# Two GNN layers on one core: h1's two right-hand products as one joint two-level product, W1 from DRAM, x1 added by the DMA

## The chip, the core and the metric

The kernel runs on one core of a Trainium2 chip. A core has TensorE (PE, matrix products into PSUM), VectorE (DVE), ScalarE (ACT), GpSimd (POOL) and SyncE (SP, which here issues most DMAs); they run their own instruction streams in program order and wait for one another by semaphores. The metric is the time of one execution in microseconds on the device (us). The kernel before was run three times: median 2367.68, from 2367.29 to 2368.17.

## The reference

Everything is fp32. There are 32 batches of 512 nodes with 512 features, an adjacency `adj` (512x512 per batch) and a node mask.

```python
h = relu(layernorm(x))                       # over the features
deg = adj.sum(-1)
agg = adj @ h / max(deg, 1e-6)
x1 = x + relu(concat(h, agg) @ W.T)          # W: 512 x 1024
h1 = relu(layernorm(x1))
q, k = split(h1 @ Wqk)
v = h1 @ Wv
w = mask * sum(q * (adj @ (k * mask)), -1) / sqrt(512)
out = x1 + softmax(w, over the nodes) * v
```

## The kernel before, in words

**Algebra.** W is split in W1 (for h) and W2 (for agg). With A = adj/deg the kernel computes y = h·W2 and out = h·W1 + A·y. In the second layer the weights of q and k are joined before the loop, M = Wq·Wkᵀ, so that the score of a node is the dot product of a row of t = h1·M with the same row of u = A·(mask·h1), times the degree. So a batch has six 512x512x512 terms: y, h·W1, A·y, u, t and v = h1·Wv.

**Products.** Each term is a Strassen-Winograd product over 2x2 blocks of 256: seven block products, each of four matmuls of 128x128 weights with 256 moving columns (28 matmuls instead of 32). The weights come from a transposed left operand (hT, aT, h1T, sums of blocks included: seven slots), the moving columns from a right operand with seven slots. `product` (L114) is a generator that yields after each step of four matmuls per term; the matmul is L124. Its banks are pp, pr and pq. Their order: block product 1 into pp, copied by ScalarE (L91) as c11; 2 into pr, added by VectorE (L85); 6 is accumulated onto pp, hence waits for the copy of pp; then 5 into pq (copied as m5), 7 onto pp, 3 onto pq, 4 onto pp. Sums of blocks for a left or a right operand are four VectorE operations of 128x512 each (L85 add, L88 subtract). Where a result becomes the right operand of another product (y), `end` in `layer0_y` makes its sums on VectorE.

**Transposes.** A normalised row block goes to a DRAM scratch tensor, is read back so that 32-blocks lie where they are wanted, and is transposed by VectorE in 32x32 blocks (L199). This is done for h, A and h1 (classes `FrontH` L263, `FrontA` L283, `FrontH1` L310).

**Stages.** The order of the work is written out by hand: for each stage a plan lists what else is issued after which step (`at(step, f)`), and `run` (L158) takes a step of the products, then what the plan has there. A batch i has three stages: SINGLE, out(i), 14 steps; PAIR, t(i-1) and v(i-1) with steps interleaved; PAIR, y(i+1) and u(i) interleaved. The chain from out to h1 (statistics L221 and L222, variance L226, power -0.5 on POOL L227, shift L231, normalisation with ReLU on ScalarE L235, mask L331) is issued in the t/v stage. Softmax (L404 and following) with its two reductions over partitions on POOL comes in the y/u stage; there VectorE adds sm·v to x1 in the x tile (L437), and SP stores it (L444). W1, W2, M and Wv stay in SBUF as `w1R`, `w2R`, `mR`, `vR` for the whole kernel. DMAs are issued by SP, in order.

**Head and tail.** Before the loop the weights are turned, M is multiplied (`pm`), and out(0) runs; between them TensorE transposes the mask (L622). After the loop the last softmax, its additions and stores follow the last product of v.

## Time and profile before

| | |
|---|---|
| median of three runs | 2367.68 us |
| profiled execution, its own time | 2370.62 us |
| its span (first to last instruction) | 2368.8 us |
| granted TensorE clock, mean | 0.998 |
| TensorE busy | 2343.9 us |
| VectorE busy | 1491.9 us |
| ScalarE busy | 861.2 us |
| POOL busy | 91.9 us |
| moved by the SP queue | 335.74 MB, 56.2% of 16 DMA engines |
| one batch in mid-run (1072 to 1146 us and 1000 to 1072) | 72 to 74 us |
| end of the last matmul to the end of the span | about 6.9 us |

The profile is of one execution, a little apart from the median. An instruction group's row gives line, engine, operation, tile written and tiles read, shape, count, then busy time and mean ns of one, then the idle time of the engine ahead of the group and what ended it. A matmul instruction leaves two records, so that "x8" is four matmuls; their lengths overlap, and the distance of the starts is the pitch. The timeline's rows are start, length, instruction, with the idle time before it and its releaser in brackets. Of a wait for several things the row names the last.

### The profile page before, as it was taken

The page shows a single profiled execution, that of the slowest core. Times are in us where ns is not written, and L with a number is a line of the kernel's source. Part 1 is how long each engine was busy: PE and PEld are TensorE (multiplying, and loading weights), DVE is VectorE, ACT ScalarE, POOL GpSimd, SP SyncE. Part 2 cuts the span into 40 slices and gives each one's busy share as a digit, 9 for nine tenths or more (in the row PEclk, how much of TensorE's full clock was granted, in tenths as well). Part 3 has the DMA queues.
Part 4 walks back from the last instruction along what each step waited for, and adds up shares of the span by engine and source line. Part 5 has one row for each costly group of instructions (what it writes and reads, how often), then busy time and mean ns, then how long its engine had stood idle before and what let it go on. Part 6 is the DMA issues. An engine that isn't in the chain of part 4 may idle for free.

```text
span 2368.8 us, 31069 instructions
## 1 busy us (share of the span) xinstructions
PE 2343.9 (99%) x10916; PEld 2063.5 (87%) x10916; DVE 1491.9 (63%) x3132; ACT 861.2 (36%) x1555; POOL 91.9 (4%) x134
## 2 busy tenths in 40 slices
PE   6999999999999999999999999999999999999998
PEld 5988888888888888888888888888888888888887
DVE  5676665666666666666666666666666666666544
ACT  4443333343333433333433334333344333343322
POOL 0000000000000000000000000000000000000000
PEclk9999999999999999999999999999999999999999
DMA  8864656645655546556456564465564665645412
GB/s 158 217 187 122 155 152 144 158 128 131 175 146 143 139 128 161 147 141 160 128 138 171 147 145 137 124 166 143 142 159 122 147 166 146 149 133 128 116 38 69
DMA packets 363596, 337.72 MB, mean 143 GB/s; under 512 B 32656, under 2 KB 266128, under 8 KB 363440
## 3 DMA queue, kind: packets, MB, share of 16 engines
q1 hardware_dynamic: 363440, 335.74, 56.2%
q8 instruction: 86, 1.41, 0.3%
q14 instruction: 70, 0.57, 0.1%
HBM read 203.49 MB, written 132.12 MB: 142 GB/s over the span
## 4 chain that ended last, share of the span: by engine, by line
PE 97%; DMA 1%; DVE 0%; ACT 0%; SPq 0%; POOL 0%; issue 0%; DVEq 0%; ACTq 0%
PE pp_o L124 19%; PE pp_v L124 9%; PE pp_t L124 9%; PE pq_o L124 9%; PE pp_u L124 9%; PE pp_y L124 9%; PE pq_v L124 5%; PE pq_t L124 5%; PE pq_y L124 5%; PE pq_u L124 5%; PE pr_o L124 5%; PE pr_v L124 2%; PE pr_t L124 2%; PE pr_u L124 2%; PE pr_y L124 2%; DMA n<-in_x_dram 0%
## 5 line engine op out<-in xcount | busy, mean ns | idle before, releaser
L124 PE MATMUL pp_o<-w1R,hT 128*128 128x256 f32 x1024 | 243.4, 381 | 0.0
L124 PE MATMUL pp_y<-w2R,hT 128*128 128x256 f32 x1024 | 242.5, 380 | 0.0
L124 PE MATMUL pp_t<-mR,h1T 128*128 128x256 f32 x1024 | 241.9, 379 | 0.0
L124 PE MATMUL pp_o<-y,aT 128*128 128x256 f32 x1024 | 241.9, 379 | 0.0
L124 PE MATMUL pp_v<-vR,h1T 128*128 128x256 f32 x1024 | 241.9, 379 | 0.0
L124 PE MATMUL pp_u<-h1m,aT 128*128 128x256 f32 x1024 | 241.9, 379 | 0.0
L124 PEld LDWEIGHTS pp_o<-w1R,hT 128*128 128x128 f32 x1024 | 195.4, 191 | 26.8
L124 PEld LDWEIGHTS pp_y<-w2R,hT 128*128 128x128 f32 x1024 | 194.9, 191 | 26.4
L124 PEld LDWEIGHTS pp_u<-h1m,aT 128*128 128x128 f32 x1024 | 194.6, 190 | 26.5
L124 PEld LDWEIGHTS pp_t<-mR,h1T 128*128 128x128 f32 x1024 | 194.6, 190 | 26.5
L124 PEld LDWEIGHTS pp_v<-vR,h1T 128*128 128x128 f32 x1024 | 194.6, 190 | 26.5
L124 PEld LDWEIGHTS pp_o<-y,aT 128*128 128x128 f32 x1024 | 194.5, 190 | 26.4
L91 ACT ACTIVATE o<-pp_o 128x512 f32<-128x512 f32 x96 | 57.3, 597 | 371.8 <-PE pp_o L124 371.8
L235 ACT ACTIVATE h1m<-x,nmr,rstd 128x512 f32<-128x512 f32 x128 | 99.9, 806 | 171.9 <-DVE nmr L231 171.9
L91 ACT ACTIVATE v<-pp_v 128x512 f32<-128x512 f32 x128 | 75.5, 590 | 223.5 <-PE pp_v L124 223.5
L91 ACT ACTIVATE y<-pp_y 128x512 f32<-128x512 f32 x128 | 76.4, 597 | 205.6 <-PE pp_y L124 205.6
L199 DVE STREAM_TRANSPOSE aT<-saT 128x1024 f32<-128x1024 f32 x62 | 77.2, 1245 | 114.3 <-DMA saT<-daT 92.6
L91 ACT ACTIVATE u<-pp_u 128x512 f32<-128x512 f32 x128 | 76.2, 595 | 141.2 <-PE pp_u L124 141.2
L227 POOL TENSOR_TENSOR rstd<-rstd,mhalf 128x4 f32<-128x4 f32 x64 | 66.6, 1040 | 1553.2 <-ACT m_o L91 913.5
L124 PE MATMUL pq_y<-w2R,hT 128*128 128x256 f32 x512 | 121.1, 379 | 0.1
L124 PE MATMUL pq_t<-mR,h1T 128*128 128x256 f32 x512 | 121.0, 379 | 0.0
L124 PE MATMUL pq_o<-y,aT 128*128 128x256 f32 x512 | 121.0, 379 | 0.0
(115 smaller groups left out, 3753.0 us busy)
## 6 DMA issues: line engine op xcount, KB each, us to landing
x<-in_x_dram SPq DMA_DIRECT2D x128, 256.0 KB, 5.6
a<-in_adj_dram SPq DMA_DIRECT2D x256, 128.0 KB, 3.1
dh1T<-h1m SPq DMA_DIRECT2D x128, 256.0 KB, 2.5
sh1T<-dh1T SPq DMA_DIRECT2D x256, 128.0 KB, 3.5
out_dram<-x SPq DMA_DIRECT2D x256, 128.0 KB, 2.3
n<-in_x_dram SPq DMA_DIRECT2D x248, 128.0 KB, 4.7
daT<-a SPq DMA_DIRECT2D x124, 256.0 KB, 2.0
dhT<-n SPq DMA_DIRECT2D x124, 256.0 KB, 2.0
```

The source lines that it names most:

```text
L91: nc.scalar.activation(o, i, AF.Copy)
L124: nc.tensor.matmul(p[:, rc, :], lt[:, LEFT[k], dk, ts(rc, P)], rt[:, RIGHT[k], dk, :], start=first and n == 0, stop=True, skip_group_check ...
L199: nc.vector.transpose(o, t.rearrange("p k (c r) -> p k c r", r=R))
L227: nc.gpsimd.tensor_tensor(rstd, rstd, mhalf, op=ALU.pow)
L235: nc.scalar.activation(o, i, AF.Relu, scale=t[1][:, c:c + 1], bias=t[2][:, c:c + 1])
```

## The change

- **Joint product.** t and v are computed by `layer1_tv`: the right operand `mvR` has M and Wv side by side, 128 columns each, in blocks of 128, and the algorithm is applied twice, 7 x 7 block products of 128. Each is one matmul of 128x128 weights with 256 columns (128 of M, 128 of Wv). An outer block product fills four PSUM banks (two inner products each, one in the last); ScalarE and VectorE gather the outer sums from the banks into a tile TV, where the seven inner products of each block are still apart. h1T gets the sums of the inner level too (`inner_sums`, VectorE).
- **Recombination.** In the next stage VectorE combines the inner products by seven adds of 128x1024 (`recombine`) and makes four dot products (`dot`) of 128x512.
- **Output.** ScalarE multiplies v by the softmax weight into a tile of the tag n (`apply`), POOL issues a DMA that adds x1 from DRAM to it (`store`, two of 512 KB per batch), and SP stores it with four DMAs each. x1 is put into DRAM by `keep` (1 MB, SP).
- **W1** is kept in DRAM and loaded per batch, seven DMAs of 256 KB, three tiles (`Stream`).
- **Buffers and engines.** hT is one constant tile; aT and x have one buffer instead of two, n two instead of three, tmp four instead of five. The left sums of A and the right sums of y are made by POOL.
- **Order.** Products run one after the other: out(i) 14 steps, y(i+1) 7 steps, u(i) 7 steps, joint product tv(i) 14 half steps. The rest of the chain to h1 (`chain`) is issued in y(i+1), four masks and the reading back included; the softmax of the batch before is issued in out(i). In the last batch there is no y, and `chain` is issued alone.
- **Head.** The mask's transposes by TensorE come in the stage in which M is multiplied, and y(1) and out(0) come with other loads beside them.

The diff, cut to its core, with the indentation reduced by four. Of the old stages, described above, only removed functions are shown.

```diff
--- before.py
+++ after.py
 ...
 def block(name):
-    return big.tile([P, 2, H], F32, tag="tmp", bufs=5, name=name)
+    return big.tile([P, 2, H], F32, tag="tmp", bufs=4, name=name)
 ...
+def add(o, a, b, on=None):
+    (on or nc.vector).tensor_tensor(o, a, b, op=ALU.add)
+def sub(o, a, b, on=None):
+    (on or nc.vector).tensor_tensor(o, a, b, op=ALU.subtract)
 ...
+def left_sums(s, on=None):
     return [
-        lambda: add(s(4), s(2), s(3)), lambda: sub(s(6), s(0), s(2)),
-        lambda: sub(s(5), s(4), s(0)), lambda: sub(s(2), s(1), s(5)),
+        lambda: add(s(4), s(2), s(3), on), lambda: sub(s(6), s(0), s(2), on),
+        lambda: sub(s(5), s(4), s(0), on), lambda: sub(s(2), s(1), s(5), on),
     ]
 ...
+def variance(t, a=0, b=C):
     mv, rstd, nmr = t
-    nc.vector.tensor_scalar(rstd, mv[:, :, 1], LN_EPS, None, op0=ALU.add)
-    nc.gpsimd.tensor_tensor(rstd, rstd, mhalf, op=ALU.pow)
-def shift(t):
+    nc.vector.tensor_scalar(rstd[:, a:b], mv[:, a:b, 1], LN_EPS, None, op0=ALU.add)
+    nc.gpsimd.tensor_tensor(rstd[:, a:b], rstd[:, a:b], mhalf[:, a:b], op=ALU.pow)
+def shift(t, a=0, b=C):
 ...
+    def keep(self):
+        nc.sync.dma_start(out=self.x1.rearrange("c p f -> p c f"), in_=X[self.b])
 ...
+    def masked_sums(self, i):
+        right_sums(of(H1M[self.b]))[i]()
+    def turn(self, h):
+        if h == 0:
+            H1T[self.b] = big.tile([P, 7, 7, P], F32, tag="h1T", bufs=1, name=f"h1T_{self.b}")
+        for a in range(2):
+            self.to.turn_slot(h, a, H1T[self.b][:, 2 * h + a, 0:4, :].rearrange("p i f -> p (i f)"))
     def sums(self, i):
-        right_sums(H1M[self.b])[i]()
+        left_sums(lambda s: H1T[self.b][:, s, 0:4, :])[i]()
+    def inner_sums(self, i, a, b):
+        swap = {0: 0, 1: 2, 2: 1, 3: 3, 4: 4, 5: 5, 6: 6}
+        left_sums(lambda s: H1T[self.b][:, a:b, swap[s], :])[i]()
 ...
+    def load(self):
+        k = ORDER[self.n % 7]
+        t = big.tile([P, 2, H], F32, tag="w1", bufs=3, name=f"w1_{self.n}")
+        nc.sync.dma_start(out=t, in_=self.d[RIGHT[k]])
+        self.tiles.append((k, t))
+        self.n += 1
 ...
-    place, finish = into(y)
-    def end(r, c, o, p, s):
-        finish(r, c, o, p, s)
-        t = right_sums(y)
-        if (r, c) == (0, 1):
-            for f in t[:3]:
-                f()
-        elif (r, c) == (1, 0):
-            t[3]()
-    return product(f"y_{b}", [(HT[b], w2R)], place, end)
-def layer0_out(b):
+    return product(f"y_{b}", [(hT, right(w2R))], *into(y))
+def layer0_out(b, w1):
     def place(r, c):
         return block(f"o_{b}_{r}{c}")
@@ -370,52 +431,103 @@
             p = o
         nc.vector.scalar_tensor_tensor(dst, p, 0.0, dst, op0=ALU.max, op1=ALU.add)
-    return product(f"o_{b}", [(HT[b], w1R), (AT[b], Y[b])], place, finish)
+    return product(f"o_{b}", [(hT, w1), (AT_[b], right(Y[b]))], place, finish)
 ...
-def layer1_t(b):
 ...
-        for rc in range(2):
-            nc.vector.scalar_tensor_tensor(
-                o[:, rc, :], p[:, rc, :], 1.0, U[b][:, 2 * r + c, rc, :],
-                op0=ALU.mult, op1=ALU.mult,
-                accum_out=acc[:, c, 2 * r + rc:2 * r + rc + 1],
-            )
-    return product(f"t_{b}", [(H1T[b], mR)], place, finish)
-def layer1_v(b):
-    v = V[b] = big.tile([P, 4, 2, H], F32, tag="v", bufs=1, name=f"v_{b}")
-    return product(f"v_{b}", [(H1T[b], vR)], *into(v))
 ...
+    return product(f"u_{b}", [(AT_[b], right(H1M[b]))], *into(u))
+def layer1_tv(b):
+    t = TV[b] = big.tile([P, 4, 2, 7, P], F32, tag="h1m", bufs=1, name=f"tv_{b}")
+    left = H1T[b]
+    def m(k, banks, first):
+        for half in ((2, 1), (3, 0)):
+            for n in half:
+                if first:
+                    banks[n] = mm_tile(f"ptv_{b}_{k}_{n}")
+                for i, p in enumerate(range(2 * n, min(2 * n + 2, 7))):
+                    j = AT[p]
+                    nc.tensor.matmul(
+                        banks[n][:, :, ts(i, P)],
+                        left[:, LEFT[k], LEFT_IN[j], :],
+                        mvR[:, RIGHT[k], RIGHT[j], :, :],
+                        start=first and i == 0,
+                        stop=True,
+                        skip_group_check=True,
+                    )
+            yield half
 ...
+    def keep(o):
+        return lambda n, p: copy(part(o, n), p)
+    def plus(o):
+        return lambda n, p: add(part(o, n), p, part(o, n))
+    pp, pr, pq, m5 = {}, {}, {}, {}
+    def keep5(n, p):
+        m5[n] = block(f"m5_tv_{b}_{n}")[:, :, 0:P * min(2, 7 - 2 * n)]
+        copy(m5[n], p)
+    yield from parts(1, pp, True, keep(0))
+    yield from parts(2, pr, True, plus(0))
+    yield from parts(6, pp, False, keep(1))
+    yield from parts(5, pq, True, keep5)
+    yield from parts(7, pp, False, keep(3))
+    for n in range(4):
+        add(part(3, n), part(3, n), m5[n])
+    yield from parts(3, pq, False, plus(1))
+    yield from parts(4, pp, False, keep(2))
 ...
+    def recombine(self, i, first=0, end=4, a=0, b=2):
+        def s(j):
+            t = TV[self.b][:, first:end, a:b, PLACE[j], :]
+            return t.rearrange("p o a f -> p (o a) f") if b - a == 2 else t[:, :, 0, :]
+        o, x1, x2 = [(2, 1, 2), (1, 1, 6), (5, 1, 5), (3, 5, 3), (6, 1, 7), (7, 5, 7), (4, 6, 4)][i]
+        add(s(o), s(x1), s(x2))
 ...
+    def dot(self, c):
+        v = self.row(c, 0)
+        u = U[self.b][:, 2 * (c // 2):2 * (c // 2) + 2, c % 2, :]
+        nc.vector.scalar_tensor_tensor(
+            v, v, 1.0, u, op0=ALU.mult, op1=ALU.mult, accum_out=self.acc[:, c:c + 1]
+        )
 ...
     def apply(self, c):
-        o = X[self.b][:, c, :].rearrange("p (a f) -> p a f", a=2)
-        nc.vector.scalar_tensor_tensor(
-            o, V[self.b][:, 2 * (c // 2):2 * (c // 2) + 2, c % 2, :], self.sm[:, c:c + 1], o,
-            op0=ALU.mult, op1=ALU.add,
+        h = c // 2
+        if c % 2 == 0:
+            self.n[h] = half_tile(f"out_{self.b}_{h}")
+        nc.scalar.activation(
+            self.n[h][:, c % 2, :].rearrange("p (a f) -> p a f", a=2), self.row(c, 1), AF.Copy,
+            scale=self.sm[:, c:c + 1],
         )
     def store(self, h):
+        nc.gpsimd.dma_start(
+            out=self.n[h], in_=self.f1.x1[2 * h:2 * h + 2].rearrange("c p f -> p c f"), accum_op=ALU.add
+        )
         for q, dst in enumerate(by_rows(out[self.b])):
             nc.sync.dma_start(
-                out=dst[:, 2 * h:2 * h + 2, :], in_=X[self.b][q * R:(q + 1) * R, 2 * h:2 * h + 2, :]
+                out=dst[:, 2 * h:2 * h + 2, :], in_=self.n[h][q * R:(q + 1) * R, :, :]
             )
 ...
+def chain(p, f, n):
+    p.at(n(0), f.stats, 2)
+    p.at(n(0), shift, f.t, 0, 2)
+    p.at(n(0), f.write, 0)
+    p.at(n(1), f.stats, 3)
+    p.at(n(1), variance, f.t, 2, 4)
+    p.at(n(1), f.write, 1)
+    p.at(n(2), shift, f.t, 2, 4)
+    p.at(n(3), f.write, 2)
+    p.at(n(3), f.mask, 0)
+    p.at(n(4), f.write, 3)
+    p.at(n(4), f.keep)
+    p.at(n(4), f.mask, 1)
+    p.at(n(4), f.to.read, 0)
+    p.at(n(5), f.masked_sums, 0)
+    p.at(n(5), f.mask, 2)
+    p.at(n(6), f.mask, 3)
+    p.at(n(6), f.to.read, 1)
 ...
+        m = held["pmk"] = mm_tile("pmk").rearrange("p a f -> p (a f)")[:, 0:C * B].rearrange("p (c b) -> p c b", c=C)
+            nc.tensor.transpose(m[:, c, :], mask_by[:, ts(c, P)], identity[:B, :B])
 ...
+    p.at(2, mask_turn)
+    p.at(4, mask_keep)
+        p.at(3 * d, multiply, d)
+        p.at(1 + 3 * d, place, d, 1, wvN[:, d, :])
+        p.at(3 * d + 3, lambda d=d: place(d, 0, held["m", d].rearrange("p a f -> p (a f)")))
+    chain(p, f, lambda k: 2 * k)
+    p.at(1, fh.turn, 0)
+    p.at(3, fh.turn, 1)
+    for k in range(4):
+        p.at(4 + k, fh.sums, k)
+    for k in range(3):
+        p.at(13, f.masked_sums, k + 1)
+    run(None, 14, p)
 ...
+    weights, mvR = start()
+    post = None
+    for i in range(B):
+        if i > 0:
+            p = Plan()
+            for k in range(7):
+                p.at([0, 0, 1, 2, 3, 4, 5][k], post.recombine, k)
+            for c in range(C):
+                p.at(5 + (c + 1) // 2, post.dot, c)
+            p.at(7, post.scores)
+            p.at(8, post.maximum)
+            p.at(9, post.exponents)
+            p.at(10, post.row_sum)
+            p.at(11, post.weights)
+            for c in range(C):
+                p.at(12 + c // 2, post.apply, c)
+            p.at(12, post.store, 0)
+            p.at(13, post.store, 1)
+            for n in range(4):
+                p.at(2 * n + 1, stream.load)
+            if i + 1 < B:
+                fb = FA[i + 1]
+                for h in range(2):
+                    for c in range(2):
+                        p.at(3 * h + c, fb.sum, 2 * h + c)
+                        p.at(3 + 3 * h + c, fb.write, 2 * h + c)
+                    p.at(2 + 3 * h, fb.degrees, h)
+                th = FH[i + 1]
+                p.at(2, th.to.read, 0)
+                p.at(4, th.to.read, 1)
+                p.at(8, th.turn, 0)
+            f = F1[i] = FrontH1(i)
+            p.at(12, f.stats, 0)
+            p.at(12, f.stats, 1)
+            p.at(13, variance, f.t, 0, 2)
+            if i + 1 < B:
+                p.at(13, th.turn, 1)
+                p.at(13, th.sums, 0)
+                p.at(13, th.sums, 2)
+            run(layer0_out(i, stream.take), 14, p)
+            p = Plan()
+            chain(p, f, lambda k: k)
+            if i + 1 < B:
+                p.at(2, th.sums, 1)
+                p.at(2, th.sums, 3)
+            run(layer0_y(i + 1) if i + 1 < B else None, 7, p)
+        else:
+            f = F1[0]
+            p = Plan()
+            for k, g in enumerate(weights):
+                p.at(min(k, 6), g)
+            run(layer0_y(1), 7, p)
+        p = Plan()
+        if i > 0:
+            for k in range(3):
+                p.at(0, f.masked_sums, k + 1)
+        p.at(1, f.turn, 0)
+        p.at(3, f.turn, 1)
+        for k in range(4):
+            p.at([2, 2, 3, 6][k], f.inner_sums, k, 0, 2)
+            p.at(4 + k // 2, f.sums, k)
+        p.at(6, f.inner_sums, 0, 2, 7)
+        if i + 1 < B:
+            p.at(2, FA[i + 1].to.read, 0)
+            p.at(3, FA[i + 1].to.read, 1)
+        if i + 2 < B:
+            fh = FH[i + 2] = FrontH(i + 2)
+            p.at(3, fh.load, 0)
+            p.at(4, fh.load, 1)
+        run(layer1_u(i), 7, p)
+        p = Plan()
+        for k in range(1, 4):
+            p.at(k - 1, f.inner_sums, k, 2, 7)
+        if i + 1 < B:
+            fb = FA[i + 1]
+            p.at(1, fb.turn, 0)
+            p.at(2, fb.turn, 1)
+            for k in range(4):
+                p.at(3 + k, fb.sums, k)
+                p.at(7 + k, right_sums(of(Y[i + 1]), nc.gpsimd)[k])
+            p.at(3, load_x, i + 1)
+            for n in range(3):
+                p.at(8 + 2 * n, stream.load)
+        if i + 2 < B:
+            for c in range(C):
+                p.at(5 + c, fh.stats, c)
+                p.at(9 + c, fh.write, c)
+            p.at(8, variance, fh.t)
+            p[9].insert(0, lambda t=fh.t: shift(t))
+            fa = FA[i + 2] = FrontA(i + 2)
+            p.at(12, fa.load, 0)
+            p.at(13, fa.load, 1)
+        post = Post(i, f)
+        if i + 1 == B:
+            for n, o in ((10, 0), (11, 3), (12, 1)):
+                for k in range(7):
+                    p.at(n, post.recombine, k, o, o + 1)
+            p.at(13, post.dot, 0)
+            p.at(13, post.dot, 1)
+        run(layer1_tv(i), 14, p)
+    for k in range(7):
+        post.recombine(k, 2, 3, 0, 1)
+    post.dot(2)
+    post.dot(3)
+    post.scores()
+    post.maximum()
+    for k in range(4):
+        post.recombine(k, 2, 3, 1, 2)
+    post.exponents()
+    post.row_sum()
+    for k in range(4, 7):
+        post.recombine(k, 2, 3, 1, 2)
+    post.weights()
     for c in range(C):
+        post.apply(c)
+        if c % 2:
+            post.store(c // 2)
```

## The prediction

> **What bounds the kernel now.** I read the profile's first part, then the chain that ended last. Both say the same thing.

> ```profile
> span 2368.8 us, 31069 instructions
> ...
> PE 2343.9 (99%) x10916; PEld 2063.5 (87%) x10916; DVE 1491.9 (63%) x3132; ACT 861.2 (36%) x1555; POOL 91.9 (4%) x134
> ...
> PE 97%; DMA 1%; DVE 0%; ACT 0%; SPq 0%; POOL 0%; issue 0%; DVEq 0%; ACTq 0%
> ```

> The matmuls fill the span and no other engine appears in the chain, so a matmul fewer is worth its full pitch, as long as nothing new makes TensorE wait. The timeline gives the pitch. Columns: start, length, instruction; "x8" is the records of the four matmuls of one step.

> ```profile
> 1047.77 1.89 PE L124 MATMUL pr_o<-w1R,hT 128*128 128x256 f32 x8
> 1049.50 1.89 PE L124 MATMUL pr_o<-y,aT 128*128 128x256 f32 x8
> 1051.23 1.89 PE L124 MATMUL pp_o<-w1R,hT 128*128 128x256 f32 x8
> ```

> A step starts every 1.727 us, so a matmul costs 0.432 us. A batch has 168 of them: 72.5 us. VectorE works 46.6 of each batch's 73 us (mean of two mid-run windows). What a delay of the engines behind TensorE looks like is in the groups and on VectorE's timeline.

> ```profile
> L235 ACT ACTIVATE h1m<-x,nmr,rstd 128x512 f32<-128x512 f32 x128 | 99.9, 806 | 171.9 <-DVE nmr L231 171.9
> L91 ACT ACTIVATE y<-pp_y 128x512 f32<-128x512 f32 x128 | 76.4, 597 | 205.6 <-PE pp_y L124 205.6
> L227 POOL TENSOR_TENSOR rstd<-rstd,mhalf 128x4 f32<-128x4 f32 x64 | 66.6, 1040 | 1553.2 <-ACT m_o L91 913.5 <-DVE rstd L226 639.6
> ```

> The first row: ScalarE's normalisation of h1 stands idle 171.9 us in 32 batches (5.4 us each) for the shift that VectorE makes, and this costs nothing today, since every product runs beside a second one (t beside v, y beside u).

> ```profile
> 1051.50 0.69 DVE L85 TENSOR_TENSOR o<-pr_o,o 128x512 f32<-128x512 f32 x1 [0.86 <-PE pr_o L124]
> 1052.22 0.69 DVE L371 SCALAR_TENSOR_TENSOR x<-o,x 128x512 f32<-128x512 f32 x1
> 1052.83 0.68 DVE L85 TENSOR_TENSOR aT<-aT 128x512 f32<-128x512 f32 x1
> ...
> 1056.03 0.69 DVE L221 BATCH_NORM_STATS2 st<-n 128x6 f32<-128x512 f32 x1
> 1056.76 0.18 DVE L222 BATCH_NORM_AGGREGATE mv<-st 128x2 f32<-128x6 f32 x1
> 1056.93 0.69 DVE L221 BATCH_NORM_STATS2 st<-n 128x6 f32<-128x512 f32 x1
> ```

> These give the durations that I use: 0.60 us from one 128x512 operation to the next, 0.73 if it needs the one before, 0.72 from statistics to aggregate, 0.17 on from there. A step's end reaches VectorE 0.27 us later (1051.23 to 1051.50) and ScalarE 0.20 later.

> [...] after an idle 3.63 us, the four microseconds from 44 ran at 0.65.

> ```profile
> 43.42 0.60 PE L622 MATMUL pmk<-identity,mask_by 32*128 32x32 f32 x4 [3.63 <-DVE mask_by L615]
> ```

> [...]

> **The change part by part.**

> *Removed.* t and v, 56 matmuls, become 49: 7 x 32 x 0.432 = **-96.7 us**, if the pitch stays. The output of a matmul becomes two strided runs of 128 columns; I take no cost for it.

> *The chain of h1 after out, now under y(i+1) alone.* Call E the start of y's first matmul, out's end. Order on each engine is that of the program. VectorE: out's last but one step ends at E-3.45, so the add to o01 is at -3.18, the ReLU-add (L432) -2.46, statistics 0 -1.73, aggregate -1.00, statistics 1 -0.84, aggregate -0.11, variance 0.09, transpose of hT's second half 0.20 (1.245 long), hT sums 1.49 and 2.22, the last ReLU-add 2.82, statistics 2 3.55, aggregate 4.27, shift 4.4. Then ScalarE: normalisation 0 at 4.6 (0.72), and behind it in its order the copy of y's first bank (called at L144, helper L100), 5.33 to 5.93. TensorE's third y product adds into that very bank, so it waits: it starts at 5.99 instead of 3.45. The stall is 2.55 us; with a few hundredths for the semaphores in between I take 2.6: x30 batches (the first and the last are made differently) = **+78 us**. [...] The bounds: if VectorE did the transpose and the sums before out ends (they only need the second half of hT to land), 0 to 0.5 us; if the half lands a microsecond late, 3.6. In the old order steps of t and v stood between.

> *What is queued behind it.* Later copies follow at their own distances, and normalisation 2 needs statistics 3, one POOL power (1.04) and a shift, due near E+7.7 when ScalarE is at its step there; no second wait.

> *Joint product.* VectorE loses 8 dot halves (0.42), 8 transposed-sum and 8 Y/aT operations (to POOL), and 4 apply operations (0.74; to ScalarE), and gains inner sums, seven 128x1024 recombinations and wide adds out of PSUM: 46.6 becomes about 54 to 58 us of a batch of 70 to 72. By phases: out 23.8 of 24.2, y 6.5 of 12.1, u 12.1 of 12.1, joint product 16.2 of 21.1. The slack at the joint product's bank adds is about 2 us, at inner sum 3 1.7 us. Costed at nothing; if this cover goes, each late microsecond costs 31 us.

> *POOL.* [...] the second half of y's sums is needed only by out, ten steps later.

> *DMAs.* W1's blocks add 1.84 MB, the kept x1 1.05, the accumulating read 1.05 to 2.1: 10.5 MB per batch (335.74/32) becomes 14.4 to 15.5, at today's 56.2% scaled 77 to 83% busy. W1's loads are three blocks ahead, 3 to 5 us before use. On SP, in order: the accumulating DMA, then four stores that wait for it, then the first row write of h1 (L366), for which mask 0 waits on ScalarE. It holds without new stall if the accumulation takes up to 5.5 us[...].

> *Last batch.* No y remains beneath the chain: The last shift comes about E+5, two normalisations make 6.5, the landing of a row store (2.5 us for dh1T in the profile) 9.0, two masks of 0.6 to 0.7 10.4: TensorE idles so long and then loses 1.5 us by a lower clock as in the head[...]: 12.7. *Tail.* After the last matmul now 6.9 us; after the change bank copies 2.2, last recombinations 2.9, dots and scores 2.4, two reductions 1.6, exp, sum, weights 1.2, four applies 2.9, [...]stores 4.6, some waits 3: 27, +20. *Head.* The mask's transposes move to where the weights are multiplied: -3.6 idle, -1.5 clock, -0.5; new first transposes +2.

> Sum against the profiled span: 2368.8 - 96.7 + 78 + 12.7 + 20 - 5.6 + 2 = 2379.2. The median shown, 2367.68, lies 1.1 under the span (the profiled run itself took 2370.62): **2378 us**, slower by 0.45%.

> **The rivals.** *A: the stall is hidden* (chance 0.14). Then the 96.7 go through but for last batch and tail: 2300. For it: ScalarE is at 36%, and the chain needs only VectorE to be two steps earlier; against it: VectorE runs its instructions in program order, and at out's end ten of them stand ahead of the shift. The change is faster than 0.2% from a stall under 2.05 us on; at 1.3 us it is 2340. *B: the accumulation is late* (0.16). [...]the first write of h1 lands 2.6 us later, mask 0 stands ahead of a bank copy, and every batch loses up to 2.6 more: 2378 to 2458. For it: DMA share near 80%; against: it decides only above 5.5 us. *C: DMA or VectorE are full* (0.14). Loads or wide adds late by 1.5 us per batch: 2425. *D: more than one of these[...]* (0.04): over 2460. The main case has 0.52.

> **How the numbers follow.** The main case alone: the stall can be 2.0 to 3.3, so 2360 to 2400. About 0.2% (4.7 us) is what a measurement here can tell. Faster by that: A, and little of the main case, 0.16. Within it, 2363 to 2372.4: main's lower end, 0.10. Slower: 0.74. The range must reach part of A (2325) and most of B and C (2450).

> **What would show it.** In the profile after: an idle of about 2.6 us of TensorE once per batch before the third product of y, released by ScalarE's copy at L100, and ScalarE waiting for the shift ahead of it; the matmul mean still 380 ns; VectorE near 75%; DMA near 200 GB/s; a tail of 27 us. I am wrong if TensorE waits instead at the joint product's banks (C), if masks wait for dh1T (B), or if the idle is under 1 us (A).

## The result

| | before | changed |
|---|---|---|
| median of four runs | 2367.93 us | 2688.09 us |
| range | 2367.29 to 2369.91 | 2681.87 to 2690.23 |
| span of the profiled execution | 2368.8 us | 2686.6 us |
| mean granted TensorE clock | 0.998 | 0.940 |

The ratio is 1.1346, 95% interval 1.1326 to 1.1366: slower by 13.5%, where 0.45% was forecast. The page of the changed kernel, its head, its engines and its chain that ended last:

```profile
span 2686.6 us, 32248 instructions
...
PE 2336.3 (87%) x10372; PEld 2012.5 (75%) x10372; DVE 1815.7 (68%) x3296; ACT 1111.4 (41%) x2035; POOL 495.6 (18%) x478
...
PE 52%; DVE 13%; issue 10%; DMA 10%; POOL 7%; ACT 6%; SPq 2%; ACTq 0%; DVEq 0%; POOLq 0%
```

TensorE is no longer busy all the time, and a tenth of the chain is "issue": time in which an engine waited for nothing that the profile shows. Most of what TensorE waits sits in one place. Its timeline of one batch shows it (start, length, instruction, then the idle time before it and its releaser):

```profile
1212.56 1.89 PE L130 MATMUL pp_y<-w2R,hT 128*128 128x256 f32 x8
1214.29 1.89 PE L130 MATMUL pr_y<-w2R,hT 128*128 128x256 f32 x8
1224.44 3.78 PE L130 MATMUL pp_y<-w2R,hT 128*128 128x256 f32 x8 [8.26 <-ACT y L100]
1228.01 2.26 PE L130 MATMUL pq_y<-w2R,hT 128*128 128x256 f32 x8
```

It is the place of the forecast, y's third product waiting for ScalarE's copy of the first bank. But the wait is 8.26 us and not 2.6, and the step behind it takes 3.78 instead of 1.89. Over the kernel these waits sum to 250.2 us in 30 batches. On ScalarE the copy stands behind the normalisation, and that behind VectorE's shift:

```profile
1223.09 0.81 ACT L252 ACTIVATE h1m<-x,nmr,rstd 128x512 f32<-128x512 f32 x1 [11.57 <-DVE nmr L246]
1223.81 0.57 ACT L100 ACTIVATE y<-pp_y 128x512 f32<-128x512 f32 x1
...
1212.50 0.27 DVE L241 TENSOR_SCALAR rstd<-mv 128x2 f32<-128x2 f32 x1
1212.70 1.25 DVE L274 STREAM_TRANSPOSE hT<-shT 128x1024 f32<-128x1024 f32 x1
...
1216.03 0.69 DVE L236 BATCH_NORM_STATS2 st<-x 128x6 f32<-128x512 f32 x1
1216.76 0.18 DVE L237 BATCH_NORM_AGGREGATE mv<-st 128x2 f32<-128x6 f32 x1
1222.83 0.16 DVE L246 SCALAR_TENSOR_TENSOR nmr<-mv,rstd 128x2 f32<-128x2 f32 x1 [5.89 <-POOL rstd L242]
```

VectorE came to the shift 4.4 us after y's start, as worked out in the prediction (1216.94 against 1212.56). It then stood 5.89 us for POOL's power. On POOL:

```profile
1208.07 0.39 POOL L541 PARTITION_ALL_REDUCE gs<-es  x1 [4.48 <-DVE es L540]
1210.59 2.62 POOL L557 DMA_DIRECT2D out<-dx  x2 [2.13 <-ACT out L551]
1222.07 0.73 POOL L242 TENSOR_TENSOR rstd<-rstd,mhalf 128x2 f32<-128x2 f32 x1 [8.86 <-issue]
```

The variance was there at 1212.77. The power ran 9.3 us later, 8.86 us behind the two DMA issues (8.2 to 9.9 over the batches), and the profile shows nothing in between. The question for the experiments was what holds POOL in these 8.86 us.

### The profile page after: what moved, and what is told of

It is laid out like the page before. It is cut to its first block, busy times and chain, and to the rows that moved or that the text cites. A ratio compares the mean times of both kernels' runs of the same rounds, so it can differ in the third digit from the quotient of the medians.

```text
span 2686.6 us, 32248 instructions
## 1 busy us (share of the span) xinstructions
PE 2336.3 (87%) x10372; PEld 2012.5 (75%) x10372; DVE 1815.7 (68%) x3296; ACT 1111.4 (41%) x2035; POOL 495.6 (18%) x478
## 3 DMA queue, kind: packets, MB, share of 16 engines
q0 software_dynamic: 17408, 33.56, 7.8%
## 4 chain that ended last, share of the span: by engine, by line
PE 52%; DVE 13%; issue 10%; DMA 10%; POOL 7%; ACT 6%; SPq 2%; ACTq 0%; DVEq 0%; POOLq 0%
PE ptv L453 10%; PE pp_o L130 8%; PE pq_o L130 8%; PE pp_y L130 8%; PE pp_u L130 7%; DMA a<-in_adj_dram 5%; PE pq_y L130 4%; PE pq_u L130 4%; POOL aT L97 3%; DMA dhT<-n 3%; DVE st L236 2%; PE pr_u L130 2%; POOL rstd L242 2%; DVE x L432 1%; DVE hT L274 1%
## 5 line engine op out<-in xcount | busy, mean ns | idle before, releaser
L453 PE MATMUL ptv<-mv,h1T 128*128 128x256 f32 x3136 | 682.9, 379 | 0.5 <-DVE h1T L97 0.4
L453 PEld LDWEIGHTS ptv<-mv,h1T 128*128 128x128 f32 x3136 | 595.6, 190 | 82.6 <-DVE h1T L97 2.0
L130 PE MATMUL pp_y<-w2R,hT 128*128 128x256 f32 x1024 | 298.4, 443 | 250.2 <-ACT y L100 250.2
L100 ACT ACTIVATE tv<-ptv 128x512 f32<-128x512 f32 (+1 forms) x512 | 256.9, 540 | 185.2 <-PE ptv L453 185.1
L94 DVE TENSOR_TENSOR tv<-tv 128x1024 f32<-128x1024 f32 (+2 forms) x252 | 274.2, 1102 | 8.4 <-ACT tv L100 1.0
L130 PE MATMUL pp_o<-w,hT 128*128 128x256 f32 x992 | 238.7, 383 | 36.3 <-ACT o L100 31.9
L130 PEld LDWEIGHTS pp_o<-w,hT 128*128 128x128 f32 x992 | 185.0, 190 | 76.6 <-ACT o L100 43.9
L130 PEld LDWEIGHTS pp_u<-h1m,aT 128*128 128x128 f32 x1024 | 195.5, 191 | 42.8 <-ACT h1m L369 16.2
L100 ACT ACTIVATE u<-pp_u 128x512 f32<-128x512 f32 x128 | 76.4, 597 | 255.1 <-PE pp_u L130 255.1
L97 DVE TENSOR_TENSOR h1T<-h1T 128x256 f32<-128x256 f32 (+2 forms) x288 | 179.2, 631 | 1.1
L279 DVE STREAM_TRANSPOSE h1T<-sh1T 128x512 f32<-128x512 f32 x128 | 83.4, 690 | 121.8 <-DMA sh1T<-dh1T 120.9
L97 POOL TENSOR_TENSOR y<-y 128x512 f32<-128x512 f32 x124 | 156.1, 1270 | 2.4
L324 ACT ACTIVATE a<-a 128x512 f32<-128x512 f32 x128 | 79.2, 619 | 173.3 <-DMA a<-in_adj_dram 173.0
```

Of the source, the lines that this page charges most:

```text
L94: (on or nc.vector).tensor_tensor(o, a, b, op=ALU.add)
L97: (on or nc.vector).tensor_tensor(o, a, b, op=ALU.subtract)
L100: nc.scalar.activation(o, i, AF.Copy)
L130: nc.tensor.matmul(p[:, rc, :], lt[:, LEFT[k], dk, ts(rc, P)], right[:, dk, :], start=first and n == 0, stop=True, skip_group_check=True,)
L279: nc.vector.transpose(o, self.s[h][:, :, ts(a, 2 * R)].rearrange("p k (c r) -> p k c r", r=R))
L324: nc.scalar.activation(v, v, AF.Copy, accum_out=DEG[self.b][:, c:c + 1])
```

## The experiments

Excess time per batch below is the mean distance from one batch's first y matmul to the next, less 161 matmuls of 0.4316 us (69.49). The changed kernel has 81.92, so an excess of 12.4 us. In the diffs "..." stands for other lines, and the comments behind "#" are notes.

### Four first runs: the order of POOL and ScalarE, the kind and the shape of the DMA

e1 moves the accumulations behind the two powers and the stores into u:

```diff
-                p.at(12, post.store, 0)      # out(i): accumulate and store
-                p.at(13, post.store, 1)
 ...
                 chain(p, f, lambda k: k)     # y(i+1)
+                p.at(2, post.accumulate, 0)
+                p.at(2, post.accumulate, 1)
 ...
+                p.at(1, prev.store, 0)       # u(i)
+                p.at(2, prev.store, 1)
```

> The changed kernel with its two accumulating DMAs on POOL issued after both powers of h1's chain (in y(i+1), step 2), and the eight stores on SP in u(i), steps 1 and 2. Theory (POOL is held by making up the two DMAs; the first power stands behind them for 8.9 us): the power runs as soon as its variance is there, the wait before y's third product falls from 8.3 us to 2.6, and with it the clock loss of 2.4 us, so about 2687 - 30 x (10.6 - 2.6) = 2447 us. Rival (traffic on the DMA engines makes everything late, the power's place is not the cause): above 2640 us.

Measured: 2522.66 us, ratio 1.066 (1.0637 to 1.0683). The wait before y's third product is 2.26 us in every one of the 30 batches (67.9 us), against 2.55 worked out in the prediction: that step of it is shown. But two things were not as expected. On POOL:

```profile
1214.92 0.39 POOL L541 PARTITION_ALL_REDUCE gs<-es  x1 [4.48 <-DVE es L540]
1222.43 0.73 POOL L242 TENSOR_TENSOR rstd<-rstd,mhalf 128x2 f32<-128x2 f32 x1 [7.11 <-DVE hT L97]
1224.95 0.69 POOL L242 TENSOR_TENSOR rstd<-rstd,mhalf 128x2 f32<-128x2 f32 x1 [1.79 <-DVE rstd L241]
1225.76 2.62 POOL L557 DMA_DIRECT2D out<-dx  x2
```

The power's input was ready at 1219.53, no DMA stood ahead of it, and still it ran only at 1222.43, at a fixed distance of 6.6 to 7.4 us from the end of the reduction in all the batches. The releaser named, a sum on hT, is only the last event before it. So POOL was held without a DMA too. Secondly, 15 of the 30 waits of 2.26 us were followed by a slower clock:

```profile
2135.00:2138.41 3.41, 1.14 (x6) 1.00 0.00 0
2138.41:2141.82 3.41, 3.41 (x9) 0.50 0.63 160
...
1220.23:1223.64 3.41, 2.80 (x13) 1.00 0.00 0
1223.64:1227.05 3.41, 1.76 (x8) 1.00 0.23 77
1227.05:1230.47 3.42, 3.42 (x18) 1.00 0.90 168
```

(Two such waits, ending at 2138.18 and at 1225.29. A row is a window and its length, then how long TensorE was busy in it, then the granted clock.) The windows are not chosen freely: in the traces the granted clock changes only on a grid of 3.413 us (the 65 changes of the changed kernel, the first at 51.15, 54.56 and 156.96 us, all lie whole multiples of 3.4133 us apart), and the grid tells which waits cost. The first wait lies inside one window, which is idle for 2.27 of its 3.41 us, and the next window runs at half clock. The second wait, of the same length, is cut by a line of the grid into 0.61 and 1.65 us, and the clock stays full. So it is with all 30: the 15 waits with 2.2 us or more in one window are the 15 with a slow clock, and the other 15 have 1.9 us at most in one. Over the changed kernel and e1 to e10 (from 30 us to the last matmul), 211 windows at full clock were followed by one at half; each was idle for at least 1.88 us, and every window idle for more than 2.01 us was followed by one. In the changed kernel alone these are 32 of 683 windows at full clock, idle for 2.05 us or more, against 1.90 us at most in the other 651. This is read from the records; no run moves a wait against the grid.

The rest of the miss is in u, 31 us over its matmuls (waits of its second product for a mask, and the clock there), and in the joint product, 21 us more than in the changed kernel, which was not taken apart.

e2 is e1 with the first normalisation of h1 a step later, behind the copy:

```diff
-        p.at(n(0), f.write, 0)
+        p.at(n(1), f.write, 0)
```

> As the run above, and the first normalisation of h1 is issued a step later, so that ScalarE makes the copy of y's first bank ahead of it. Theory (what remains is ScalarE's order): the remaining 2.6 us go, about 2447 - 78 = 2369 us, with no idle time before y's third product. Rival (the wait moves to the next copy, that of y's second block, behind two normalisations): 1 to 2 us per batch come back, 2400 to 2430 us.

Measured: 2516.33 us, ratio 1.0619 (1.0602 to 1.0637). The wait before y's third product is gone, which shows that ScalarE's order made it. The time hardly moved, since the wait went elsewhere, to u's second product (86.8 us):

```profile
1150.83 0.59 PE L130 MATMUL pr_u<-h1m,aT 128*128 128x256 f32 x2
1154.08 2.74 PE L130 MATMUL pr_u<-h1m,aT 128*128 128x256 f32 x6 [2.66 <-ACT h1m L369]
```

It waits for the last mask on ScalarE, and that for the landing of h1's row in DRAM, which takes 3.0 us (median; 3.3 in e1) instead of 2.4. The accumulations now move their data in the same microseconds, which may be why: in e7 below, with the accumulations back in out, it is 2.5 us and u doesn't wait. This would be rival B's mechanism, though at another place of the accumulation.

e3 makes the two DMAs plain, e4 lays x1's scratch out in runs of 4 KB:

```diff
-                ..., accum_op=ALU.add                    # e3
 ...
-        return dram.tile([C, P, 512], ...)               # e4, for dx1 alone
+        return dram.tile([2, P, 2, 512], ...)
```

> The changed kernel with the two POOL DMAs plain, without accumulation (so x1 overwrites the weighted v: the softmax part is left out of the output). If the accumulation[...] holds POOL, the power comes within 3 us of its variance and the time is about 2450 us. If any DMA that POOL makes up holds it, nothing moves: 2670 to 2700 us, and the power still stands about 9 us behind the issue.

> The changed kernel with the x1 scratch laid out so that a partition's half is one run of 4 KB instead of two of 2 KB, on both sides of the accumulation. If the number of pieces sets how long POOL is held, the hold of 11.5 us from the first issue to the power falls to about 6, the wait before y's third product to 2.6 to 3.5 us, and the time to 2450 to 2480 us. If the bytes or a fixed cost per DMA set it, 2670 to 2700 us.

Measured: 2643.24 and 2693.29 us (one run each), against 2688.09. In both, the power stands about as far behind the last issue as before, 8.4 and 9.6 us (medians) against 8.95. e3's time lies 27 us under the range that it had for this case; the power comes 1.3 us sooner behind the reduction there (median), half of it because the issues are shorter. Plain:

```profile
1196.21 0.39 POOL L541 PARTITION_ALL_REDUCE gs<-es  x1 [4.48 <-DVE es L540]
1198.73 0.90 POOL L557 DMA_DIRECT2D out<-dx  x1 [2.13 <-ACT out L551]
1199.96 0.73 POOL L557 DMA_DIRECT2D out<-dx  x1 [0.33 <-ACT out L551]
1209.13 0.73 POOL L242 TENSOR_TENSOR rstd<-rstd,mhalf 128x2 f32<-128x2 f32 x1 [8.44 <-issue]
```

The accumulation does cost: an issue took 1.37 us instead of 0.82 (median) and the landing 6.9 us instead of 4.5 (6.4 in e4). But neither it nor the number of pieces (the queue's packets fell from 17408 to 9216 in e4) is what holds POOL.

### What holds POOL

The instructions in the order of the built program, on POOL at the end of a batch and without those for semaphores, say what the profile does not:

```
L533 ISA
L533 ISA gtop<-top 128x1
L541 ISA gs<-es 128x1
L557 DMACopy out_0<-dx 128x2x512
L557 DMACopy out_1<-dx 128x2x512
L242 ISA
L242 TensorTensor rstd<-rstd,mhalf 128x2
```

There is a bare instruction ahead of the first reduction, and another ahead of the first tensor_tensor after the reductions. The profile has no record of either. The theory was then that POOL stands at the second one: in e1 the power came 6.6 to 7.4 us behind the reduction with no DMA between them. The kernel before has the same two instructions in every batch; its power came 34 us (median) after the reductions, for a tensor that was ready only then, so a hold of 7 us would not have shown there:

```profile
1097.32 0.39 POOL L429 PARTITION_ALL_REDUCE gs<-es  x1 [3.47 <-DVE es L428]
1131.55 1.06 POOL L227 TENSOR_TENSOR rstd<-rstd,mhalf 128x4 f32<-128x4 f32 x1 [33.83 <-ACT m_o L91]
```

e5 puts a small addition directly behind the second reduction, so that the bare instruction falls ahead of the DMAs; e6 makes the reductions on TensorE and has no bare instruction in the loop:

```diff
             nc.gpsimd.partition_all_reduce(self.gs, self.es, ...)
+            nc.gpsimd.tensor_tensor(trial, mhalf, mhalf, op=ALU.add)     # e5
```

```diff
-            nc.gpsimd.partition_all_reduce(self.gtop, self.top, ..., ReduceOp.max)
+            nc.tensor.transpose(p[:1, 0:P], self.top, identity)          # e6
+            nc.vector.tensor_reduce(self.gtop[:1, :], p[:1, 0:P], AX.X, ALU.max)
 ...
+            nc.tensor.matmul(self.pg[:, 0:1], minus, self.gtop[:1, :], ...)
 ...
-            nc.gpsimd.partition_all_reduce(self.gs, self.es, ..., ReduceOp.add)
+            nc.tensor.matmul(p[:, 0:1], ones, self.es, ...)
```

> The changed kernel with a 128x4 addition on POOL directly behind the second reduction over partitions, ahead of the two DMAs. In the program a bare instruction without a record (ISA) stands ahead of each first tensor_tensor after a reduction; theory: [...]it, not the DMAs, held the power. Then the addition runs about 7 us after the reduction, the DMAs follow, and the power runs directly behind their issue, about 5.7 us after y's start instead of 9.5; wait before y's third product about 4.4 us, time about 2550 us. Rival (making up the DMAs holds POOL): the addition runs at once, the power again 8 to 9 us behind the DMAs, time 2680 us or more.

> The changed kernel with the two softmax reductions over partitions made by TensorE (a transpose of the maxima, a one-row matmul to spread them, a matmul with ones for the sum) in place of POOL; nothing else is moved. Theory[...]: no ISA is left in the loop, the power runs under 1 us after its variance though both DMAs stand ahead of it, and the wait before y's third product falls to 2.3 us; the rows of h1 may then wait on SP behind the stores (up to 4 us a batch). 2440 to 2520 us. Rival (the DMAs hold POOL): the power still comes 8 us behind them, above 2650 us.

POOL in e5:

```profile
1199.83 0.39 POOL L542 PARTITION_ALL_REDUCE gs<-es  x1 [4.47 <-DVE es L541]
1207.28 0.19 POOL L543 TENSOR_TENSOR trial<-mhalf 128x4 f32<-128x4 f32 x1 [7.07 <-issue]
1207.43 2.60 POOL L559 DMA_DIRECT2D out<-dx  x2
1209.11 1.69 POOL L243 TENSOR_TENSOR rstd<-rstd,mhalf 128x2 f32<-128x2 f32 x1
```

POOL in e6:

```profile
1239.56 2.48 POOL L572 DMA_DIRECT2D out<-dx  x2 [28.09 <-ACT out L566]
1241.54 1.25 POOL L246 TENSOR_TENSOR rstd<-rstd,mhalf 128x2 f32<-128x2 f32 x1
```

This settles it. The addition stands 7.07 us behind the reduction (6.7 to 7.8 over the batches), and the power follows the DMA issues at once; without the reductions, and so without a bare instruction in the loop, nothing stands before the power but the issues themselves. It isn't the reduction that runs on unseen, either: in the changed kernel both DMAs were issued within 5 us of its end, and the hold came behind them, where the bare instruction stands. Some 7 of the 8.86 us of the changed kernel go with this instruction, not with the making up of the DMAs. What POOL does in them the traces don't show. (The 1.8 us more than in e5 were not looked into; they appear where DMA issues stand right ahead of the bare instruction, 1.3 us with plain ones.)

The times fit less well. e5 took 2671.67 us (one run) where 2550 was expected: the wait before the third product is 4.6 us (139.1 in 30), near the 4.4 expected, but the accumulations are now issued 7.6 us behind the second reduction instead of 2.5 (1199.83 to 1207.43, 1208.07 to 1210.59), the stores and the first rows of h1 come behind them on SP, and a mask ahead of the copy of m5 makes y's sixth product wait another 2.0 us (59.9); the mean granted clock was 0.951. e6 took 2565.06 us (ratio 1.0828, 1.0807 to 1.085), 45 above its range, for the same reasons in less: 80.1 us before the third product (2.7 a batch), 29.5 before the sixth, the masks 98.6 us behind the rows' landing.

### Mending what is left

e7 is e6 with e1's later stores (the accumulations stay in out) and e2's order; e8 adds the sums of the adjacency rows three steps later and, in the last batch, VectorE's addition of x1 in the x tile:

```diff
-                            p.at(3 * h + c, fb.sum, 2 * h + c)           # e8
-                            p.at(3 + 3 * h + c, fb.write, 2 * h + c)
+                            p.at(3 + 3 * h + c, fb.sum, 2 * h + c)
+                            p.at(6 + 3 * h + c, fb.write, 2 * h + c)
```

> The run above with the stores on SP moved into u(i) and the first normalisation behind the copy of y's first bank. Theory: neither y's third product nor u waits for more than 0.5 us; 2330 to 2390 us. Rival (the accumulation's traffic delays the landing of h1's rows wherever it is): u's second product waits 2 us or more and the clock falls there, 2420 to 2510 us.

> The run above, the sums of the adjacency rows issued three steps later in out(i), and in the last batch x1 added by VectorE in the x tile (without keep and accumulation). If the run above comes to 2330 to 2390 us, this is about 35 us less (25 for the wait before out's third product, 8 for the tail): 2300 to 2355 us, faster than the kernel before.

Measured: e7 2448.28 us, ratio 1.0335 (1.0315 to 1.0356); e8 2401.73, ratio 1.0143 (1.0126 to 1.016). Neither is as good as expected. The largest wait left in e7's loop was the one before out's third product (36.5 us with one in the head), then 14.8 us for a sum of hT in y, up to 0.5 a batch; u did not wait, so the rival's mechanism was wrong too, though e7's time lies in its range. e8 took the first away (1.8 us left). The difference was 47 us, about 7 of them in the tail, where 35 was forecast. What remained in e8 was 3.19 us a batch in pieces of 0.2 to 0.9 us.

e9 tried to turn hT's second half in out's steps 9 and 10. That half is still read there by out's last two products, which in e9 read the next batch's blocks in its place:

> The combined run with the transpose of hT's second half and two of its sums on VectorE moved from the end of out(i) (step 13) to its steps 9 and 10, where VectorE idles, the other two sums to y's step 1, and the statistics, power and writes of the next h one to two steps earlier in tv(i). Theory (VectorE's order at the end of out, the prediction's step, costs what is left): the shift comes at 2 us after y's start instead of 4.5, y waits nowhere, h1's rows and u come 2 us earlier; the combined run's 3.2 us a batch over the pure matmul pitch fall to 1.5 to 2: 2345 to 2365 us. Rival (what is left is TensorE's own: three small matmuls and restarts): 2385 us or more.

It took 2417.37 us, in its rival's range, and as the edit isn't open to the kernel (hT has one buffer), it tells nothing on the forecast's step. Its joint product had an excess of 0.15 us instead of 0.67, most likely from the earlier statistics, which are what e9 changes there. e10 keeps that part, leaves the turn where it was, and changes two orders in y:

```diff
-                    p.at(5 + c, fh.stats, c)
-                    p.at(9 + c, fh.write, c)
-                p.at(8, variance, fh.t)
+                    p.at(3 + c, fh.stats, c)
+                    p.at(8 + c, fh.write, c)
+                p.at(6, variance, fh.t)
 ...
-                    p.at(2, th.sums, 1)
-                    p.at(2, th.sums, 3)
+                    p.at(1, th.sums, 1)
+                    p.at(1, th.sums, 3)
 ...
-        p.at(n(3), f.mask, 0)
-        p.at(n(4), f.mask, 1)
+        p.at(n(4), f.mask, 0)
+        p.at(n(5), f.mask, 1)
```

> The combined run (e8) with three changes of order: statistics, power and writes of the next h one to two steps earlier in tv(i) (VectorE stood 2.2 us there for a power queued behind POOL's sums), hT's last two sums in y's step 1 instead of 2, and the masks of the first two rows of h1 a step later, behind the copy of m5. hT's second half is turned at its old place. Theory (waits of 0.3 to 0.9 us behind orders on VectorE and ScalarE make the combined run's 3.2 us a batch over the matmul pitch): 1.2 to 2.0 us a batch are left, 2340 to 2365 us, faster than the kernel before. Rival (restarts and the three small matmuls of the reductions make it): 2385 us or more.

Measured: 2362.61 us over eight runs, ratio 0.9974 (0.9963 to 0.9985): the one version faster than the kernel before, by 0.26%. It lies just inside its range. Its largest waits on TensorE, and POOL at the power:

```profile
PE h L623 <- ACT h L698: 14.1, 2, 13.6
PE ptop L541 <- DVE top L534: 12.7, 1, 12.7
PE pp_u L130 <- ACT h1m L373: 10.6, 1, 10.6
PE pq_y L130 <- ACT m_y L100: 7.6, 30, 0.3
```

```profile
1219.91 1.21 POOL L572 DMA_DIRECT2D out<-dx  x1 [0.33 <-issue]
1220.66 1.21 POOL L246 TENSOR_TENSOR rstd<-rstd,mhalf 128x2 f32<-128x2 f32 x1
```

Columns of the waits: us in total, times, longest. In the loop 0.25 us a batch is left in the last row, 0.1 in smaller ones; the other three rows are the head (as in the kernel before), the tail and the last batch. The excess is 2.05 us a batch (1.2 to 2.0 was expected), some 60 us of the 97 that the fewer matmuls are worth. Only these 0.4 are waits. Half of it is in out's steps: 1.0 us a batch over its matmuls without a wait, where the changed kernel, whose out has no small matmuls, has 0.2. e8, with the same small matmuls, has 0.7. So they cost 0.5 to 0.8 us a batch by this comparison, which is the rival's part in it; the rest was not taken apart.

## Why the prediction was wrong

**The fewer matmuls: right.** The joint product's 49 matmuls took 21.15 us, 0.4316 each, with two strided runs of output as with one. The whole 96.7 us were gained, and lost again.

**The stall in y(i+1): right place and right way, size wrong by one term.** The step that failed reads "aggregate 4.27, shift 4.4. Then ScalarE". It takes the first power as done by then: I priced powers at 1.04 us, on an engine for whose sums and DMA issues I charged nothing. The power ended 10.2 us after y's start instead of before 4.4. Without that hold the wait was 2.26 us (e1) against my 2.55. What the step left out is POOL's hold at the bare instruction, about 7 us (7.07 in e5). That instruction is in the kernel before, too, where 34 us lie between the reductions and the power. Two signs were there: the bare instruction in the built program, and a row of the kernel before, in its waits of POOL, that puts 7.9 us of "issue" ahead of the first operation behind such an instruction, in the head:

```profile
POOL identity masks.py:199 <- issue: 7.9, 1, 7.9
```

The change took these 34 us away by having the power's input ready 4.3 us behind the last reduction (1208.46 to 1212.77).

**The clock: wrong.** I charged none for the stall of 2.6 us; that a stall of this length costs none was not shown by any trace. Waits of 8.3 us cost 2.4 us more each (y took 22.86 us, 10.77 over its matmuls, of which 8.34 were idle): 73 us. And in e1 half of the waits of 2.26 us cost clock as well: there 2.2 us of idle within one window of 3.413 us were enough. The measurement decides, and the allowance was wrong even for my own stall.

**What was costed at nothing.** The joint product's banks: right, 0.24 us excess a batch. POOL's sums: 1.27 us each (mean); the kernel before had shown none. VectorE: 56.7 us a batch (1815.7/32), in 54 to 58. DMA: 14.4 MB a batch (461.59/32) as worked out, 71.2% busy instead of 77 to 83, over a longer span. Not seen at all: the adjacency's row sums on ScalarE wait for their loads (173.0 us) ahead of the copy that frees out's first bank, and out's third product waits for it, 31.9 us in the loop (e8, which issues these sums later, has none of it there). A wait of the same kind, 3.0 us, came in the head.

**Accumulation.** It lands after 6.9 us (median), above the 5.5 where rival B was to decide. It didn't, because the chain was later still. With the chain mended, TensorE comes to wait for the landing of h1's rows (e2, e5, e6). In e7, which moves the stores off SP's way and changes ScalarE's order, it hardly does (8.5 us before y's sixth product); what of it the stores made was not separated.

**Last batch, tail, head.** 15.0 us idle (POOL's hold, 8.71 us there, stands in its chain, too, which has 12.07 us of "issue") and 3.3 of clock, 18.3 instead of 12.7. After the last matmul 30.7 us instead of 27. The head ended 0.3 us earlier (76.7 against 77.0 at the first matmul behind the weights' product), not 3.6: the mask's wait of 3.63 us went, and that of 3.0 us for a copy on ScalarE came in its place.

The sum: 2368.8 - 96.7 + 250.2 (third product of y) + 73.1 (clock there) + 42.0 (out, 36.1 of it waits) + 7.4 (joint product) + 18.3 (last batch) + 23.8 (tail) - 0.3 (head) = 2686.6, the measured span.

**The rivals.** A ended on the wrong side. C did not occur at the joint product's banks; late loads did cost about 1 us a batch, in out. D had 0.04. Its range came true, but by luck: its cause was more than one of B and C, and POOL's hold was no mechanism of any rival.

## What to carry to other kernels

Where a change moves an operation on POOL near a reduction over partitions, look in the built program for a bare instruction between them (ISA in the listing above), and price it at what was measured here, 7.07 us (e5) to 8.86 us (changed kernel); busy shares say nothing of it (POOL was 18% busy). When a product loses the second product that ran beside it, list what stands on each engine between two uses of one bank, for every short wait now counts (2.26 us a batch made 67.9 us in e1). A wait of 2.26 us cost 1.7 us more where it fell into one window of the clock's grid than where the grid cut it (16.30 against 14.62 us for y in e1). Take waits away in the order in which they end: e1 to e10 show the next one in line each time.
